# A four-layer graph network on one core: layer 3's algebra on VectorE, its sums in two passes, tests of adj moved

## The chip, the core and the metric

The kernel runs on one core of one Trainium2 chip. The core has five engines with instruction streams of their own: TensorE (PE: matrix products, with weight loads, PEld, beside them), VectorE (DVE), ScalarE (ACT), GpSimd (POOL) and SyncE (SP), which only starts transfers here. They meet through semaphores. Data lies in SBUF (128 partitions), products arrive in PSUM, inputs and outputs in device memory (HBM). The metric is the device time of one execution in microseconds (us); lower is better. A change counts as faster or slower when it moves the time by over 2%.

## The reference

Four layers over 4096 nodes of 64 features, each `x = x + layer(relu(layernorm(x)), adj)`. `adj` is 4096 x 4096 with about one entry in 128 set. Cut to what matters:

```python
# layer 0: a sum over the last 100 neighbours of each row, with weights that halve
rank = cumsum(mask, axis=1);  k = minimum(deg, 100);  pos = rank - (deg - k)
out0 = (mask * where(pos > 0, 0.5 ** (k - pos), 0)) @ (h @ weight) + bias
# layer 1: attention over neighbours in hyperbolic space
att = adj * sigmoid((2 + 2 * qm @ k.T) / att_scale + att_bias)
support = att @ h;  out1 = support / sqrt(clip(abs(-inner), 1e-8))
# layer 2: two gated steps (GRU), relu after each
m = adj @ (x @ W);  gi = m @ wih.T + bih;  gh = x @ whh.T + bhh
r = sigmoid(i_r + h_r);  z = sigmoid(i_z + h_z);  n = tanh(i_n + r * h_n)
x = relu((1 - z) * n + z * x)
# layer 3: a midpoint in the Poincare ball
XW = tanh(|mx| / |x| * artanh(|x|)) * mx / |mx|            # mx = x @ W
gamma = 2 / maximum(1 - sum(XW * XW), 1e-15)
num = A @ (gamma * XW);  den = A @ (gamma - 1)
mid = mobius_scalar_mul(0.5, num / den)
AXW = mobius_scalar_mul(sum(A, 1), mid)     # tanh(r * artanh(|x|)) * x / |x|
out3 = expmap0(relu(logmap0(AXW)))          # tanh(|u|) * u / |u|,  artanh(|y|) * y / |y|
```

## The kernel before

The fast path holds adj as one-byte floats in SBUF (`A8`, loaded and converted once, in layer 0, by transfers that GpSimd issues), and is right only if adj holds nothing but 0 and 1. So beside the layers it reads all of adj a second time in four-byte form and tests it, 256 blocks of 128 x 512; the number of other values becomes a flag, and if it is above 0 a slower general kernel runs afterwards.

The rows are worked on in four blocks `q` of 1024. Each engine works in program order, so the Python program plans the order itself: `Weave` keeps a book of estimated times. Products of the streams are emitted directly; the small work between layers and the tests are generators that yield one operation at a time, and after every few products `draw` issues those that the book holds ready. `work` (two pieces at a time) goes before `back` (the tests).

```python
    def pieces(self):
        return self.work[:self.width] + ([] if self.quiet else self.back)
    def force(self):
        piece = min(self.work[:self.width] or self.back, key=lambda p: self.begin(p[1]))
        self.issue(piece)
        self.draw(False)
    # in Engine.run(), when a transfer is started: its landing time in the book
    w.at[k] = max(w.t[self.e], w.t["P"]) + (8.0 if "whole" in k else 6.0 if "half" in k else 4.0), "S"
```

The tests load "halves" (128 x 512) or "wholes" (128 x 1024). `depth[0]` is how many are in flight: 1 in layer 0, 4 from layer 1; `spare[0]` allows wholes from layer 2.

```python
    def checks():
        ... # load up to depth[0] ahead; then for each block
            yield DV.scalar_tensor_tensor(a, a, 0.0, a, op0=ALU.not_equal, op1=ALU.not_equal,
                                          accum_out=odd[:, j:j + 1])
```

In layer 0 (`stream0`) TensorE counts neighbours into PSUM (`cnt`); ScalarE takes one half of every count, VectorE the other (`w`), and TensorE sums with these weights (`acc`). `root[0]` names the engine of the small statistics, GpSimd for blocks 0 to 2 and VectorE for the last. Layer 1 (`stream1`) makes scores, their sigmoid on ScalarE and the product with adj on VectorE (`sig`). Layer 2 has two steps (`layer2`), each closed by `gates`, whose end is on GpSimd:

```python
        yield GP.tensor_tensor(xT, xT, r, ALU.subtract)
        yield GP.tensor_tensor(xT, xT, z, ALU.mult)
        yield GP.tensor_tensor(xT, xT, r, ALU.add)
        yield AC.activation(xT, xT, AF.Relu)
```

After the second step `post2b` turns the result back (`ps_o`), adds it to `X[q]` and goes on to `pre3`, layer 3's source: layernorm (`h`), transpose (`ps_t`), product with W (`ps_l`), lengths, artanh, tanh, gamma, and three two-byte parts of each row's source in `S3`. Its artanh is half a logarithm, and for small arguments a polynomial on GpSimd:

```python
    def artanh(x):
        nb = x.shape[1]
        xc = stat("axc", nb)
        yield DV.tensor_scalar(xc, x, ARTANH_BOUND, None, op0=ALU.min)
        r = stat("at", nb)
        yield DV.tensor_scalar(r, xc, -1.0, 1.0, op0=ALU.mult, op1=ALU.add)
        q = yield from recip(r)
        yield DV.scalar_tensor_tensor(q, xc, 1.0, q, op0=ALU.add, op1=ALU.mult)
        low = small.tile([P, 2 * QB], I32, tag="st", name="flow")[:, :nb]
        yield DV.tensor_scalar(low, xc, 0.25, None, op0=ALU.is_lt)
        x2, p = stat("x2", nb), stat("po", nb)
        yield GP.tensor_tensor(x2, xc, xc, ALU.mult)
        yield AC.activation(q, q, AF.Ln)
        yield GP.tensor_scalar(p, x2, 1.0 / 13, 1.0 / 11, op0=ALU.mult, op1=ALU.add)
        for k in (9, 7, 5, 3, 1):
            yield GP.tensor_tensor(p, p, x2, ALU.mult)
            yield GP.tensor_scalar(p, p, 1.0 / k, None, op0=ALU.add)
        yield GP.tensor_tensor(p, p, xc, ALU.mult)
        yield DV.tensor_scalar(q, q, 0.5, None, op0=ALU.mult)
        yield DV.copy_predicated(q, low, p)
        return q
```

Layer 3's sums run over 32 blocks of columns for eight groups `u` of 512 rows; quarter `k` of the sum needs source `k`. `take3` brings a group's three parts together, `post3` closes one or two groups.

```python
    def layer3():
        late = NB - QB
        first = (0, 1, 2)
        for u in first:
            if u == 2:
                weave.until(("gates", NQ - 1), DONE)
            for k in range(NQ - 1):
                weave.until((4, k), DONE)
                sum3(u, k * QB, k * QB + QB)
        weave.until((4, NQ - 1), DONE)
        for us in ((0, 1), (2, 3), (4, 5), (6,), (7,)):
            for u in us:
                sum3(u, late if u in first else 0, NB)
            weave.add(post3([(u, take3(u)) for u in us]))
        weave.finish()
    def post3(parts3):
        nb = CB * len(parts3)
        ss, den, alpha = stat("ss", nb), stat("den", nb), stat("alpha", nb)
        part = [slice(i * CB, (i + 1) * CB) for i in range(len(parts3))]
        for h, (u, (n65, al)) in zip(part, parts3):
            sq = b2("sq")[:, :CB, :]
            yield AC.activation(sq, n65[:, :, :D], AF.Square)
            yield AC.activation(den[:, h], n65[:, :, D], AF.Copy)
            yield AC.activation(alpha[:, h], al, AF.Copy)
            yield DV.tensor_reduce(ss[:, h], sq, AX.X, ALU.add)
        sgn, a = stat("sgn", nb), stat("abs", nb)
        yield DV.tensor_scalar(sgn, den, 0.0, 2.0, op0=ALU.is_ge, op1=ALU.mult)
        yield DV.tensor_scalar(a, den, -1.0, DEN_EPS, op0=ALU.mult, op1=ALU.max)
        yield DV.tensor_tensor(den, den, a, ALU.max)
        n, nr = yield from lengths(ss)
        r = yield from recip(den)
        yield DV.tensor_tensor(n, n, r, ALU.mult)
        a = yield from artanh(n)
        yield DV.scalar_tensor_tensor(a, a, 0.5, alpha, op0=ALU.mult, op1=ALU.mult)
        yield DV.tensor_scalar(a, a, ARTANH_MAX, -ARTANH_MAX, op0=ALU.min, op1=ALU.max)
        yield DV.tensor_tensor(a, a, nr, ALU.mult)
        yield DV.scalar_tensor_tensor(a, sgn, -1.0, a, op0=ALU.add, op1=ALU.mult)
        for h, (u, (n65, al)) in zip(part, parts3):
            v = n65[:, :, :D]
            yield DV.tensor_tensor(v, v, rows(a[:, h]), ALU.mult)
            yield AC.activation(v, v, AF.Relu)
            sq = b2("sq")[:, :CB, :]
            yield AC.activation(sq, v, AF.Square)
            yield DV.tensor_reduce(ss[:, h], sq, AX.X, ALU.add)
        n, nr = yield from lengths(ss)
        yield DV.tensor_scalar(n, n, TANH_CLAMP, None, op0=ALU.min)
        yield AC.activation(n, n, AF.Tanh)
        yield DV.tensor_tensor(n, n, nr, ALU.mult)
        for h, (u, (n65, al)) in zip(part, parts3):
            v = n65[:, :, :D]
            yield DV.tensor_tensor(v, v, rows(n[:, h]), ALU.mult)
            x = X[u // 2][:, (u % 2) * CB:(u % 2 + 1) * CB, :]
            yield DV.tensor_tensor(x, x, v, ALU.add)
            yield SY.dma_start(out_nm[:, u * CB:(u + 1) * CB, :], x)
```

The main program ends with the tests that are left, then the flag, and the read of it in all engines (after the fast kernel, and before the branch to the general one):

```python
    layer3()
    while weave.back:
        weave.force()
    ... # flag_ps = odds summed over partitions, one product
    V.tensor_copy(flag, flag_ps[:1, :1])
            ...
            others = nc.values_load(flag)
            with tc.If(others > 0):
                general_kernel(tc, aps, out)
```

## Time and profile before

| what | value |
|---|---|
| time, median of 3 (lowest, highest) | 899.12 us (898.83, 900.8) |
| profiled execution: span, mean granted clock of TensorE | 897.3 us, 0.965 |
| layer 0, layer 1, layer 2 (from the rows "acc", "sig") | to 253, to 513, to 734 us |
| layer 3: last source complete, last product, end | 794.9, 857.9, 897.3 us |
| tests: halves in layers 0, 1, 2 | 21, 38, 7 |
| tests: wholes up to 735 us, to 797, to the end | 65, 16, 14 |
| read from HBM | 144.75 MB |

In the rows of the profile a line of the program is named by L and its number; since helpers record every operation, nearly all are L762 (VectorE, ScalarE, GpSimd) or L929 (products), and the tiles' names tell them apart: `A` is adj in one byte, `S` layer 3's source, `xT` the state in the gates, `po` the polynomial, `n` a group in the closing, `whole` and `half` the tests. "out<-in" gives what is written and read; the bracket at the end of a timeline row is the idle time before it and what ended it.

### The profile page before, as it was taken

Reading aid. Unit: us, or ns where it says so; the run is one execution under the profiler, and the core shown is the slowest. Engines: PE = TensorE matmul, PEld = TensorE weight load, DVE = VectorE, ACT = ScalarE, POOL = GpSimd, SP = SyncE. Lnnn points to the kernel's source line nnn. Section 1 sums busy time; section 2 is a strip of 40 time slices with the busy share of each in tenths; the row PEclk is TensorE's granted clock in tenths of the full one; section 3 lists DMA queues with packets and bytes.
Section 4 is the critical chain, followed back from the end, with each engine's and each line's share of the span. In section 5 each row is a group of like instructions: output and inputs, shape, how many; then the busy total and the mean of one; then the engine's idle time right before and its main releaser. Section 6 shows DMA issues by size and latency. Waiting matters only on the chain.

```text
span 897.3 us, 12837 instructions
## 1 busy us (share of the span) xinstructions
PE 812.4 (91%) x4682; PEld 383.4 (43%) x4682; DVE 657.2 (73%) x1456; ACT 369.1 (41%) x548; POOL 206.7 (23%) x470
## 2 busy tenths in 40 slices
PE   5999999999999999999999999899999974799920
PEld 2444444444433333333333344344444432789920
DVE  6755566665678888888888876577758788787776
ACT  4443444443455666666666510321103434322331
POOL 4342553556200000000000000422203363433121
PEclk9999999999999999999999999999999997799975
DMA  9997999999411320310311338477592432453210
GB/s 133 113 114 105 100 93 147 116 117 122 79 60 35 119 70 5 102 60 24 105 48 59 100 113 299 161 244 235 194 304 85 132 95 70 141 189 100 90 36 15
DMA packets 61702, 101.62 MB, mean 113 GB/s; under 512 B 18112, under 2 KB 34496, under 8 KB 61632
## 3 DMA queue, kind: packets, MB, share of 16 engines
q1 hardware_dynamic: 40752, 79.18, 28.4%
q0 software_dynamic: 18432, 16.79, 21.7%
q10 hardware_dynamic: 2448, 4.76, 1.4%
q8 instruction: 39, 0.64, 0.3%
q14 instruction: 31, 0.25, 0.1%
HBM read 144.75 MB, written 6.29 MB: 168 GB/s over the span
## 4 chain that ended last, share of the span: by engine, by line
PE 50%; DVE 14%; POOL 8%; ACT 3%; issue 3%; DMA 1%; POOLq 0%; DVEq 0%; ACTq 0%
PE acc L929 28%; PE score L929 13%; PE cnt L929 3%; POOL xT L762 3%; POOL po L762 3%; DVE nt L762 2%; DVE whole L762 2%; PE ps_l L929 2%; DVE ss L762 2%; DVE sig L762 1%; DVE n L762 1%; PE ps_n L929 1%; DVE ny L762 1%; PE ps_t L933 1%; POOL s3v L762 1%
## 5 line engine op out<-in xcount | busy, mean ns | idle before, releaser
L762 ACT ACTIVATE sig<-score,fatt_add,fatt_mul 128x1024 f32<-128x1024 f32 x128 | 147.6, 1200 | 84.1 <-PE score L929 84.0
L762 DVE TENSOR_TENSOR sig<-sig,A 128x1024 f32<-128x1024 f32 x128 | 151.4, 1222 | 34.6 <-ACT sig L762 34.0
L762 DVE TENSOR_SCALAR w<-cnt 128x512 int16<-128x512 f32 x128 | 88.5, 691 | 68.3 <-PE cnt L929 65.2
L762 DVE SCALAR_TENSOR_TENSOR whole<-whole 128x1024 f32<-128x1024 f32 x95 | 126.7, 1363 | 12.8 <-DMA whole<-in_adjT 12.4
L929 PE MATMUL score<-qd,kT 64*128 64x512 f32 x512 | 127.7, 616 | 0.7 <-ACT sig L762 0.4
L762 ACT ACTIVATE w<-cnt 128x512 int16<-128x512 f32 x128 | 76.4, 597 | 124.3 <-PE cnt L929 123.9
L762 POOL TENSOR_TENSOR xT<-xT,r 128x512 f32<-128x512 f32 x16 | 28.2, 1761 | 422.2 <-ACT r L762 421.7
L929 PE MATMUL acc<-sig,S 128*64 128x512 f32 x512 | 124.9, 606 | 0.3
L929 PE MATMUL acc<-A,hm 128*128 128x512 fp8e4 x512 | 117.5, 380 | 0.0
L929 PEld LDWEIGHTS <-hm 128*128 128x128 bf16 x768 | 72.3, 98 | 95.5 <-issue 17.9
L929 PE MATMUL cnt<-A,ftri 128*128 128x512 fp8e4 x256 | 98.0, 385 | 7.8 <-DMA A<-in_adjT 7.8
L929 PE MATMUL cnt<-A,fupd 128*128 128x512 fp8e4 x248 | 95.6, 386 | 5.0 <-ACT w L762 3.5
L929 PE MATMUL acc<-S,A 128*128 128x196 bf16 x1024 | 91.4, 251 | 4.9 <-POOL S L762 4.0
L929 PEld LDWEIGHTS <-A 128*128 128x128 fp8e4 x1024 | 89.5, 98 | 7.1 <-issue 6.6
L1073 POOL DMA_DIRECT2D A<-in_adjT x128 | 70.0, 559 | 48.5 <-DMA A<-in_adjT 45.6
L929 PEld LDWEIGHTS score<-qd,kT 64*128 64x128 f32 x512 | 43.9, 186 | 77.9 <-ACT sig L762 36.1
L929 PE MATMUL acc<-w,hm 128*128 128x512 bf16 x256 | 75.5, 379 | 0.0
L929 PEld LDWEIGHTS acc<-sig,S 128*64 128x64 f32 x512 | 30.4, 136 | 82.2 <-issue 31.2
L929 PE MATMUL acc<-A,lo 128*64 128x512 fp8e4 x512 | 61.3, 382 | 0.0
L929 PEld LDWEIGHTS <-lo 128*64 128x64 bf16 x768 | 35.6, 109 | 59.8 <-issue 39.6
L762 DVE SCALAR_TENSOR_TENSOR half<-half 128x512 f32<-128x512 f32 x66 | 44.0, 685 | 0.0
L929 PEld LDWEIGHTS <-fupd 128*128 128x128 bf16 x248 | 24.5, 99 | 43.5 <-issue 22.4
(194 smaller groups left out, 795.0 us busy)
## 6 DMA issues: line engine op xcount, KB each, us to landing
whole<-in_adjT SPq DMA_DIRECT2D x95, 512.0 KB, 5.4
half<-in_adjT SPq DMA_DIRECT2D x66, 256.0 KB, 3.0
A<-in_adjT POOLq DMA_DIRECT2D x128, 128.0 KB, 9.9
x<-in_x SPq DMA_DIRECT2D x8, 256.0 KB, 13.2
qs<-qd ACTq DMA_DIRECT2D x8, 256.0 KB, 5.1
qd<-qs SPq DMA_DIRECT2D x8, 256.0 KB, 2.7
mx<-gs SPq DMA_DIRECT2D x16, 128.0 KB, 6.9
xT<-gs SPq DMA_DIRECT2D x8, 256.0 KB, 6.4
```

The lines of the kernel that those rows point to most:

```text
L762: return fn(*args, **kw)
L929: nc.tensor.matmul(o, lhsT, rhs, start=start, stop=stop, skip_group_check=True)
L933: nc.tensor.transpose(o, src, ident)
L1073: nc.gpsimd.dma_start(A8[q][b // 2][:, b % 2, :], adjT[b * P:(b + 1) * P, q * 2 * CW:(q + 1) * 2 * CW])
```

## The change

It moves the work of GpSimd after layer 0's loads to VectorE: small statistics (`root[0]` stays VectorE), the end of the gates, artanh's polynomial (now of five coefficients and fused operations), and the last products of the sources. It puts table loads of ScalarE ahead of their use (`preload`). It gives the tests more transfers in flight (four halves in layer 0; four wholes and three halves from layer 2), books transfers as one queue, and holds the tests off (`quiet`) from the end of layer 2 until the second pass of the sums. Layer 3's sums go in two passes: three groups take sources 0 and 1 and are taken out of PSUM, three others take all four sources as they come, then the first three take sources 2 and 3 and the halves are added, and the last two follow alone. The closing uses that the relu can be applied before the lengths, and that expmap0 of logmap0 keeps directions: both lengths are computed at once and one chain is left of two. The flag is computed and read before the last chain is finished. It is meant to fill TensorE's waits and to shorten the closing.

```diff
         self.banks[self.kind.pop(k)].append(self.used[k][0])
+
+    def land(self, k, dur):
+
+        self.dma = max(self.dma, self.t["P"]) + dur
+        self.at[k] = self.dma + 2.4, "S"
 ...
-    def force(self):
-
-        piece = min(self.work[:self.width] or self.back, key=lambda p: self.begin(p[1]))
+    def force(self, back=False):
+
+        piece = min(self.work[:self.width] + (self.back if back else []), key=lambda p: self.begin(p[1]))
         self.issue(piece)
         self.draw(False)
 ...
+    depth = [4]
+    spare = [0]
 
     def checks():
 ...
-                if spare[0] and todo:
+            while todo or halves:
+                whole = sum(a.shape[1] > CW for a in loaded)
+                if whole < spare[0] and todo:
                     b, c = todo.pop(0)
                     load(b4p.tile([P, 2 * CW], F32, tag="b4", name="whole"), b, 2 * c, 2)
-                else:
+                elif len(loaded) - whole < depth[0]:
                     if not halves:
                         b, c = todo.pop(0)
                         halves += [(b, 2 * c), (b, 2 * c + 1)]
                     load(b2("half", (P, CW)), *halves.pop(0), 1)
+                else:
+                    break
             a, j = loaded.pop(0), n % 16
             n += 1
             yield DV.scalar_tensor_tensor(a, a, 0.0, a, op0=ALU.not_equal, op1=ALU.not_equal,
 ...
 
-                if c == 0:
+                if c == 0 or b % 2 == 0:
                     S_.activation(wt[:, cols[c]], cnt[c], AF.Relu, scale=-128.0)
                 else:
 ...
             for bs in pieces[-1:] if q < 2 else pieces:
                 sum2(accs[q], layer, q, bs)
+            if step and q == NQ - 1:
+                weave.quiet = True
             take2(q, step, accs.pop(q))
             weave.add(post(q))
 ...
         free(rz[0])
         yield AC.activation(r, r, AF.Tanh, bias=gb[:, 2:3])
-        yield GP.tensor_tensor(xT, xT, r, ALU.subtract)
-        yield GP.tensor_tensor(xT, xT, z, ALU.mult)
-        yield GP.tensor_tensor(xT, xT, r, ALU.add)
-        yield AC.activation(xT, xT, AF.Relu)
+        yield DV.tensor_tensor(xT, xT, r, ALU.subtract)
+        yield DV.tensor_tensor(xT, xT, z, ALU.mult)
+        yield DV.tensor_tensor(xT, xT, r, ALU.add)
         return xT
 ...
         ps = yield PE([o], run, 0.6, [kind])
-        yield DV.tensor_tensor(X[q], X[q], blocks(ps), ALU.add)
+        yield DV.scalar_tensor_tensor(X[q], blocks(ps), 0.0, X[q], op0=ALU.max, op1=ALU.add)
         free(ps)
         yield from pre3(q, kind)
 ...
 # artanh2 (artanh's lines are printed above; new order of Ln and the polynomial)
         q = yield from recip(r)
         yield DV.scalar_tensor_tensor(q, xc, 1.0, q, op0=ALU.add, op1=ALU.mult)
+        yield AC.activation(q, q, AF.Ln)
+        yield from preload(AF.Tanh)
         low = small.tile([P, 2 * QB], I32, tag="st", name="flow")[:, :nb]
         yield DV.tensor_scalar(low, xc, 0.25, None, op0=ALU.is_lt)
         x2, p = stat("x2", nb), stat("po", nb)
+        yield DV.tensor_tensor(x2, xc, xc, ALU.mult)
+        yield DV.tensor_scalar(p, x2, *(2.0 * c for c in ARTANH_POLY[:2]), op0=ALU.mult, op1=ALU.add)
+        yield DV.tensor_tensor(p, p, x2, ALU.mult)
+        for c in ARTANH_POLY[2:-1]:
+            yield DV.scalar_tensor_tensor(p, p, 2.0 * c, x2, op0=ALU.add, op1=ALU.mult)
+        yield DV.scalar_tensor_tensor(p, p, 2.0 * ARTANH_POLY[-1], xc, op0=ALU.add, op1=ALU.mult)
+        yield from between
         yield DV.copy_predicated(q, low, p)
         return q
 
 ... # pre3: preload(AF.Ln) before the lengths; its four GP operations are DV
 # layer3, summed (layer3 of before is printed above)
     def layer3():
+
+        half = NB // 2
+        sets = (0, 1, 2), (3, 4, 5)
+        early = {}
+        for k in range(2):
+            for place, u in enumerate(sets[0]):
                 weave.until((4, k), DONE)
+                sum3(u, place, k * QB, k * QB + QB)
+                if k:
+                    early[u] = take3(u)
+        for lo, hi in ((0, 1), (1, 2), (2, 3), (3, 4)):
+            for place, u in enumerate(sets[1]):
+                weave.until((4, lo), DONE)
+                sum3(u, place, lo * QB, hi * QB)
+                if hi == NQ:
+                    summed(u, take3(u))
+        weave.quiet = False
+        for place, u in enumerate(sets[0]):
+            sum3(u, place, half, NB)
+            summed(u, take3(u, early.pop(u)))
+        for place, u in enumerate((6, 7)):
+            sum3(u, place, 0, NB)
+            summed(u, take3(u), alone=True)
+        while weave.back:
+            weave.force(True)
+        others = nc.values_load(flag)
         weave.finish()
+        return others
+
+    pair = []
+
+    def summed(u, parts3, alone=False):
+        pair.append((u, parts3))
+        if alone or len(pair) == 2:
+            weave.add(post3(pair[:]))
+            pair.clear()
 ...
+        if more is not None:
+            V.tensor_tensor(n65, n65, more[0], ALU.add)
+            V.tensor_tensor(alpha, alpha, more[1], ALU.add)
 ... # post3, the new lines only
+        sgn, den, ss = stat("sgn", nb), stat("den", nb), stat("ss", 2 * nb)
+        vs = [n65[:, :, :D] for u, (n65, al) in parts3]
+        for h, v, (u, (n65, al)) in zip(part, vs, parts3):
+            d = n65[:, :, D]
+            yield DV.tensor_scalar(sgn[:, h], d, 0.0, 2.0, op0=ALU.is_ge, op1=ALU.mult)
+            yield DV.scalar_tensor_tensor(v, rows(sgn[:, h]), -1.0, v, op0=ALU.add, op1=ALU.mult)
+            sq = b2("sq")
+            yield AC.activation(sq[:, :CB, :], v, AF.Square)
+            yield DV.scalar_tensor_tensor(sq[:, CB:, :], v, 0.0, v, op0=ALU.max, op1=ALU.mult)
+            yield DV.tensor_scalar(den[:, h], d, -1.0, DEN_EPS, op0=ALU.mult, op1=ALU.max)
+            yield DV.tensor_tensor(den[:, h], den[:, h], d, ALU.max)
+            yield DV.tensor_reduce(ss.rearrange("p (k b) -> p k b", k=2)[:, :, h],
+                                   sq.rearrange("p (k b) d -> p k b d", k=2), AX.X, ALU.add)
+        yield from preload(AF.Ln)
+        rd = yield from recip(den)
+        n, r = yield from lengths(ss)
+        t = stat("t", nb)
+        yield DV.tensor_tensor(t, n[:, :nb], rd, ALU.mult)
+        ratio = stat("ratio", nb)
+        def between():
+            yield DV.tensor_tensor(ratio, n[:, nb:], r[:, :nb], ALU.mult)
+            for h, v in zip(part, vs):
+                yield DV.scalar_tensor_tensor(v, v, 0.0, rows(r[:, nb:][:, h]), op0=ALU.max, op1=ALU.mult)
+        a = yield from artanh2(t, between())
+            yield DV.scalar_tensor_tensor(a[:, h], a[:, h], 0.25, al, op0=ALU.mult, op1=ALU.mult)
+        yield DV.scalar_tensor_tensor(a, a, ARTANH_MAX, ratio, op0=ALU.min, op1=ALU.mult)
+        yield AC.activation(a, a, AF.Tanh)
+        for h, v, (u, (n65, al)) in zip(part, vs, parts3):
+    weave.dma = 5.2
 ...
-        root[0] = GP if q < NQ - 1 else DV
-    spare[0] = True
+    depth[0], spare[0] = 3, 4
 ... # flag_ps, its product and copy move to the end of checks()
+    others = layer3()
+    return others
```

## The prediction

> **What bounds the kernel now.** I read the busy shares and the forty slices first, to see which stage is not filled; then a table by stage; then, where TensorE is not filled, its instructions in order of time, and after its last product VectorE's. On the page:
>
> ```profile
> PE 812.4 (91%) x4682; PEld 383.4 (43%) x4682; DVE 657.2 (73%) x1456; ACT 369.1 (41%) x548; POOL 206.7 (23%) x470
> PE   5999999999999999999999999899999974799920
> DVE  6755566665678888888888876577758788787776
> PEclk9999999999999999999999999999999997799975
> DMA  9997999999411320310311338477592432453210
> ```
>
> TensorE is at 9 until slice 32 (layers 0, 1 and the first part of layer 2), so nothing there can bring much unless it shortens TensorE's own work, and the change does not. It falls to 7, 4, 7 at about 720 to 790 us and to 2, 0 in the last 40 us. The clock row falls with it. The same four stages as a table (layer 2; layer 3's sources; its sums; the closing):
>
> ```profile
> 513.00:734.00 221.00, 212.89 (x1234) 93.39 (x1232) 156.54 (x322) 50.38 (x81) 52.29 (x61) 0.99 0.58 188
> 734.00:797.00 63.00, 39.92 (x363) 35.07 (x362) 52.38 (x138) 20.59 (x38) 28.11 (x48) 0.81 0.38 125
> 797.00:858.00 61.00, 60.81 (x713) 60.55 (x711) 44.11 (x183) 18.68 (x61) 13.26 (x39) 1.00 0.36 116
> 858.00:897.30 39.30, 0.19 (x2) 0.11 (x2) 26.45 (x127) 10.89 (x21) 5.71 (x26) 0.55 0.07 15
> ```
>
> Columns after the length: busy time of TensorE, weight loads, VectorE, ScalarE, GpSimd, then clock, DMA share, GB/s. TensorE idles 23 us of 63 in the sources and is slowed besides (clock 0.81), is full in the sums, and has nothing in the last 39 us. So there are two holes. The first, in TensorE's own order:
>
> ```profile
> 754.12 1.11 PE L933 MATMUL ps_o<-fident,xT 128*128 128x128 f32 x4 [5.34 <-ACT xT L762]
> 765.79 1.11 PE L933 MATMUL ps_t<-fident,h 128*128 128x128 f32 x4 [10.56 <-DVE h L762]
> 768.12 0.81 PE L929 MATMUL acc<-S,A 128*128 128x196 bf16 x4 [1.22 <-POOL S L762]
> ```
>
> It waits for the chain of the last block of rows (q=3): gates, layernorm, source. The chain of waits there alternates between VectorE and GpSimd, with tests of adj ("whole") in between. The page names GpSimd's part:
>
> ```profile
> L762 POOL TENSOR_TENSOR xT<-xT,r 128x512 f32<-128x512 f32 x16 | 28.2, 1761 | 422.2 <-ACT r L762 421.7
> L762 DVE SCALAR_TENSOR_TENSOR whole<-whole 128x1024 f32<-128x1024 f32 x95 | 126.7, 1363 | 12.8 <-DMA whole<-in_adjT 12.4
> ```
>
> The second hole is the closing: after TensorE's last product at 857.9 two chains run almost one after the other, to the last update of X at 885.7, and only then come the last tests, the flag and the read of it:
>
> ```profile
> 885.27 0.42 DVE L762 TENSOR_TENSOR X<-X,n 128x256 f32<-128x256 f32 x1
> 889.44 1.22 DVE L762 SCALAR_TENSOR_TENSOR whole<-whole 128x1024 f32<-128x1024 f32 x1
> 891.45 0.15 DVE L762 CAST flag<-flag_ps 1x1 int32<-1x1 f32 x1 [0.37 <-PE flag_ps L1656]
> ```
>
> From the last X to the end (897.3) are 11.6 us: 5.2 of tests, 0.7 of flag, 5.7 for reading the flag in every engine and the branch.
>
> **What the Trainium skill says.** "SBUF — State Buffer", section Who interferes with whom: a VectorE instruction with two SBUF inputs and a GpSimd instruction that reads SBUF share one port pair, and one waits for the other's whole length; tensor_scalar can take the pair too, in its two-port modes. The trace agrees: a test takes 1.22 us when GpSimd is still and up to 2.28 beside it (748.7 us), one 16-element tensor_scalar on VectorE takes 1.26 instead of 0.17 (752.2 us), GpSimd's small ones 1.1 to 1.3 instead of 0.2. "ScalarE: Activation LUTs", section What ACT_TABLE_LOAD costs: a change of table set takes about 1283 ns. The trace has 1.28 us for each, some of them in front of a Tanh that a chain waits for. "TensorE: Matmul & The Clock Gate", section What's actually happening: an idle array falls to half clock. The clock here is 0.81 in the sources and 0.55 in the closing.
>
> **The change part by part.**
>
> *Layers 0 and 1 (to 513 us).* In layer 0 half of VectorE's evictions of the counts (64 of 0.69 us) go to ScalarE (0.60 each), and the small statistics of three blocks of rows come from GpSimd to VectorE, some 47 operations of 0.2 us each block: -33 us (the three blocks with tests) and +28, even. TensorE is full (182.6 busy of 186 us from 67 to 253), so the length stays. What changes is the tests: 21 halves there now, one in flight; with four in flight I estimate 30 more. VectorE idles 73 us of those 186, and 30 take 30x0.69=21. For DMA: A's tiles follow each other every 1.25 us where nothing else loads (GpSimd's issues from 42 to 57 us), and TensorE uses one each 1.83 us, so a half (about 0.62 by its size) fits into two blocks of three and more. Layer 1 has VectorE at 220 of 260 us and keeps its 38 halves. Sum: 0, give or take 3 us.
>
> *Layer 2 (513 to 734).* The gates' three operations leave GpSimd (1.27 to 2.1 us each) for VectorE (0.69, as its other 128x512 ones): about 3 us less in each of eight chains. TensorE waits on that result 4.9 us (ps_l) and 2.4 (ps_o before 740); I take 4 back, so the sums end near 730. VectorE idles 65 us here; gates for seven chains take 7x3x0.69=14.5, the first two sources some 12. Half of the remaining 38, at 1.23 a test, is 15 more tests. So of the 30 "whole" now tested after 735 us, 15 are gained in layer 0 (30 halves) and perhaps 11 to 15 here; I take four as left, 5 us.
>
> *Layer 3's sources.* The chain of q=3 takes from 734 to 794.9 us now (last S part). In the new one I count: take and gates 6.7 us, GRU end 2.1, ps_o and X 1.3, layernorm 5.6, transpose, product and copies 2.7, squares 2.0, lengths 2.4, artanh with its polynomial (7x0.2 instead of 13 GpSimd steps of 0.3) 2.6, tanh to factors 2.3, S 3.2. Sum 31; with another block's operations between, 35. No tests are in it. So the last source is ready near 765.
>
> *The sums.* TensorE has 1024 products at 88.8 ns (216 in 19.17 us) = 91 us, plus 9 us for projections and transposes. Before, three groups waited for sources 0 to 2 before the first could be closed; now three groups take the first two sources, three others all four as they come: 17+25=42 us of products that do not need q=3. From 730 that is work until 781, later than 765. The hole closes, and TensorE ends near 730+9+91=830 instead of 857.9.
>
> *The closing.* A pair's algebra is 36 small operations at 0.2 us and per half six large ones (five of 0.44, one of 0.70): 7.2+5.8=13.0 us of VectorE. Before: 42 small ones and 4.3 large, 12.7. It is the chain that is shortened (one chain of lengths, no GpSimd polynomial, no second Square), not VectorE's work. A single group is about 9.3, eleven takings with their additions 10.5. Sum: 3x13.0+2x9.3+10.5=68 us, which start when group 3 is complete, at 730+9+17+34-5.7=784. That gives 852, against 830+1.6+10.5=842 from TensorE's end. VectorE, not TensorE, sets the end. Some of it overlaps: before, 53.8 us were busy where this count gives 58 (0.17 for 0.2), so 63 to 68: 847 to 852. I take 850.
>
> *The end.* Tests left 5, waiting for the flag in the last chain 2, and after the last X its output and the branch 4 to 5 (an estimate: of the 11.6 now, without tests and most of the read). 850+5+2+5=862.
>
> **The rivals.** (1) Tests stay over: if layer 0's loads find less room, VectorE in the tail gets up to 15 tests more, 18 us: 880. For it: the DMA share is already 0.87 there. Against: the 1.25 us above. (2) Layer 0's larger test loads delay A's tiles and TensorE waits: 5 to 10 us, 870. Against: tiles are issued twelve ahead and land in 9.9 us, the twelve last 22. GpSimd with no arithmetic left also issues them in time. (3) Banks: the last chains need one and two-bank buffers that the new groups hold from their start; if gates of q=3 come after the third group has taken its bank they wait 17 us, the hole stays, 878. Against: TensorE's first two groups last 5.7 us and the gates are ready 2.2 us after the sums. (4) VectorE overlaps better than counted, and no test is left: TensorE's end plus the last chain bounds, 842+5: 848.
>
> **Range and chances.** 862 is 4.1% below the time before, on the profile's scale; the timed median is 1.8 above its span, inside my error. The low end is rival 4, the high end rival 1 or 3 in full: 848 to 880. Faster by over 2% means under 881: 0.85; the rest is two rivals together: same 0.11, slower 0.04.
>
> **What would show it.** Right: TensorE without a wait over 2 us between 730 and 830 and clock near 1 there; no GpSimd arithmetic; VectorE near full from 785 to the end; the flag's copy before the last X. Wrong: a long wait of TensorE for h or xT after 740 (step of the sources), "A" among TensorE's waits in layer 0, over ten tests after 785, or VectorE with much idle in the closing (then its chains, not its work, set the end).

## The result and the profile after

| | before | after |
|---|---|---|
| time, median (lowest, highest) | 899.33 us (898.83, 900.8), 4 runs | 848.85 us (848.38, 850.1), 4 runs |
| ratio, 95% interval | | 0.9438 (0.9422 to 0.9455) |
| profiled span, granted clock of TensorE | 897.3 us, 0.965 | 846.8 us, 0.988 |
| TensorE: products of layer 1 end, of layer 2, of layer 3 | 514.3, 734.0, 857.8 us | 516.6, 727.5, 821.8 us |
| last source complete, last update of X starts | 793.7, 885.3 us | 771.5, 839.6 us |
| tests left when the closing starts or later | 14 wholes that end after 797 us | 1 whole, 1 half |

The kernel is 50.5 us faster: 36.0 us up to the end of TensorE's products, and 14.5 us after it. (The last source of before is complete at 793.7 us; the 794.9 of the table of before is 1.2 us too late.) The page first, its busy line and the forty slices:

```profile
PE 803.9 (95%) x4682; PEld 378.5 (45%) x4682; DVE 644.0 (76%) x1670; ACT 397.8 (47%) x609; POOL 69.5 (8%) x143
PE   5999999999998999999999999999999999999980
DVE  6725766667667888888888888977678788885996
PEclk9999999999999999999999999999999999999995
DMA  9999999999641041032022133796778920000010
```

The hole at slices 33 to 35 is gone, TensorE is at 9 from slice 14 to slice 38, and its clock falls only in the last slice. GpSimd fell from 206.7 us of busy time to 69.5, nearly all in layer 0. VectorE is not busier than before (644.0 against 657.2 us) although it took over GpSimd's work: 64 evictions of layer 0 went to ScalarE (397.8 us busy against 369.1), and the tests became shorter. DMA moves its load to slices 26 to 32, where four wholes are in flight.

By stage: layer 2, the sources beside the first sums, the closing beside the last sums, and what follows TensorE's last product (columns as before):

```profile
513.00:728.00 215.00, 213.60 (x1255) 94.08 (x1252) 171.56 (x418) 52.06 (x87) 0.46 (x4) 1.00 0.63 206
728.00:777.00 49.00, 48.98 (x540) 46.07 (x538) 36.02 (x136) 21.67 (x48) 0.48 (x4) 1.00 0.01 2
777.00:822.00 45.00, 44.83 (x527) 44.60 (x524) 38.91 (x179) 17.12 (x52) 0.00 (x0) 1.00 0.06 14
822.00:846.80 24.80, 0.19 (x2) 0.09 (x2) 16.59 (x83) 7.28 (x15) 0.00 (x0) 0.59 0.10 25
```

TensorE lacks 0.02 us of 49 and 0.17 of 45. The last 24.8 us are what remains of the second hole. TensorE's own order, where the three waits of before (5.34, 10.56 and 1.22 us) stood:

```profile
740.88 0.60 PE L951 MATMUL ps_o<-fident,xT 128*128 128x128 f32 x4
...
749.14 0.60 PE L951 MATMUL ps_t<-fident,h 128*128 128x128 f32 x4
...
752.54 69.29 PE L947 MATMUL acc<-S,A 128*128 128x196 bf16 x812
840.31 0.19 PE L947 MATMUL flag_ps<-fones,odds 128*1 128x1 f32 x2 [18.48 <-DVE odds L780]
```

No row has a bracket until the flag's product. 812 products in 69.29 us are 85.3 ns each. The two groups that stood for GpSimd and for the tests (the first from the tile's view: durations as lowest, median and highest ns, then first and last start):

```profile
L780 DVE TENSOR_TENSOR xT<-xT,r x16: 675/692/693, 566.5 to 739.0; 128x512 f32<-128x512 f32 x16
```

```profile
L780 DVE SCALAR_TENSOR_TENSOR whole<-whole 128x1024 f32<-128x1024 f32 x53 | 63.5, 1219 | 4.9 <-DMA whole<-in_adjT 4.3
```

The gates' operation takes 0.69 us where it took 1.76 on average on GpSimd. A whole test takes 1.22 us on average where it took 1.36. The shorter test fits what the Trainium skill says in "SBUF — State Buffer", section Who interferes with whom: a VectorE instruction with two SBUF inputs, as the test is, contends with a GpSimd instruction that reads SBUF. The run gates_pool below puts such instructions back and shows the difference. Last, VectorE around the closing:

```profile
770.62 0.83 DVE L780 TENSOR_TENSOR S<-s3v,S 128x260 bf16<-128x260 f32 x2
777.29 0.62 DVE L780 TENSOR_TENSOR n<-n,acc 128x130 f32<-128x130 f32 x2 [5.84 <-ACT alpha L780]
...
835.34 1.22 DVE L780 SCALAR_TENSOR_TENSOR whole<-whole 128x1024 f32<-128x1024 f32 x1
...
838.50 0.68 DVE L780 SCALAR_TENSOR_TENSOR half<-half 128x512 f32<-128x512 f32 x1
...
839.56 0.42 DVE L780 TENSOR_TENSOR X<-X,n 128x256 f32<-128x256 f32 x1
...
840.54 0.15 DVE L780 CAST flag<-flag_ps 1x1 int32<-1x1 f32 x1 [0.28 <-PE flag_ps L947]
```

Three things are to be seen. VectorE has nothing to do for 5.84 us just before the closing starts. Two tests lie in the middle of the last chain. The flag's copy comes after the last X, so the read of the flag is not ahead of anything.

### The profile page after: what moved, and what is told of

Same layout as the page of the kernel before. It is cut to its first block, busy times and chain, and to the rows that moved or that the text cites. A ratio compares the mean times of both kernels' runs of the same rounds, so it can differ in the third digit from the quotient of the medians.

```text
span 846.8 us, 12798 instructions
## 1 busy us (share of the span) xinstructions
PE 803.9 (95%) x4682; PEld 378.5 (45%) x4682; DVE 644.0 (76%) x1670; ACT 397.8 (47%) x609; POOL 69.5 (8%) x143
## 4 chain that ended last, share of the span: by engine, by line
PE 86%; DVE 7%; DMA 2%; ACT 2%; issue 1%; POOL 0%; POOLq 0%; ACTq 0%; DVEq 0%
PE acc L947 50%; PE score L947 14%; PE cnt L947 13%; PE ps_l L947 2%; PE ps_t L951 2%; PE rz L947 2%; DMA half<-in_adjT 2%; PE ps_n L947 2%; PE ih L947 1%; DVE sig L780 1%; DVE n L780 1%; DVE nt L780 1%; DMA A<-in_adjT 1%; PE ps_kq L947 1%; DVE rc L780 1%
## 5 line engine op out<-in xcount | busy, mean ns | idle before, releaser
L780 ACT ACTIVATE w<-cnt 128x512 int16<-128x512 f32 x192 | 108.1, 595 | 95.9 <-PE cnt L947 93.8
L780 DVE SCALAR_TENSOR_TENSOR half<-half 128x512 f32<-128x512 f32 x150 | 98.3, 683 | 2.6 <-DMA half<-in_adjT 2.6
L947 PE MATMUL acc<-S,A 128*128 128x196 bf16 x1024 | 88.5, 247 | 0.0
L947 PEld LDWEIGHTS <-A 128*128 128x128 fp8e4 x1024 | 87.2, 97 | 1.5 <-issue 1.0
L780 DVE TENSOR_SCALAR w<-cnt 128x512 int16<-128x512 f32 x64 | 44.2, 690 | 50.9 <-PE cnt L947 49.8
L1104 POOL DMA_DIRECT2D A<-in_adjT x128 | 67.7, 531 | 138.5 <-DMA A<-in_adjT 135.1
L780 DVE SCALAR_TENSOR_TENSOR whole<-whole 128x1024 f32<-128x1024 f32 x53 | 63.5, 1219 | 4.9 <-DMA whole<-in_adjT 4.3
## 6 DMA issues: line engine op xcount, KB each, us to landing
A<-in_adjT POOLq DMA_DIRECT2D x128, 128.0 KB, 12.7
```

The source lines that it names most:

```text
L780: return fn(*args, **kw)
L947: nc.tensor.matmul(o, lhsT, rhs, start=start, stop=stop, skip_group_check=True)
L1104: nc.gpsimd.dma_start(A8[q][b // 2][:, b % 2, :], adjT[b * P:(b + 1) * P, q * 2 * CW:(q + 1) * 2 * CW])
```

## The experiments

Each one alters the changed kernel unless it says otherwise. The ratios are to the kernel before, timed on the same chip; the differences in us are to 848.85 (the kernel before differs by up to 0.5 us between these chips). The first six put one part of the change back, or give it to the engine that had it.

### one_pass: the sums in the order of before

```diff
-        for k in range(2):            # groups 0-2: sources 0, 1; groups 3-5: all four; ...
+        for u in (0, 1, 2):           # groups 0-2: sources 0, 1, 2; then each group to its end
+            ... sum3(u, place(u), k * QB, k * QB + QB)   # k = 0, 1, 2
+        weave.quiet = False           # after the last source
+        for us in ((0, 1), (2, 3), (4, 5), (6,), (7,)): ...
```

> The changed kernel with the order of layer 3's sums of before: groups 0 to 2 take sources 0 to 2, then all wait for source 3, then (0,1), (2,3), (4,5), 6, 7. Everything else as changed. Theory 'order' (the two passes fill TensorE): group 0 has only 5.7 us of products before it needs source 2, which is complete at 761, so TensorE idles about 20 us between 741 and 761 and the time is 868 to 874. Rival 'chains' (the sources are now so quick that any order is filled): TensorE idles under 6 us and the time is under 855.

Measured: 855.15 us, ratio 0.9504 (0.9488 to 0.9519), +6.3 us. The hole is back in TensorE's order:

```profile
739.77 0.63 PE L951 MATMUL ps_o<-fident,xT 128*128 128x128 f32 x4 [0.61 <-DVE xT L780]
751.68 6.45 PE L947 MATMUL acc<-S,A 128*128 128x196 bf16 x40 [11.28 <-DVE S L780]
...
776.10 0.19 PE L947 MATMUL flag_ps<-fones,odds 128*1 128x1 f32 x2
776.22 61.80 PE L947 MATMUL acc<-S,A 128*128 128x196 bf16 x724
```

TensorE ends at 838.0, 16 us later, yet the time grows by only 6.3. What came between is seen after TensorE's end: here the last X ends at 848.4, 10.4 us after the last product; in the changed kernel it ends 18.2 us after it. With TensorE late, VectorE has no backlog (45.0 us busy of the 61 before TensorE's end), and the last group's chain runs alone: 40 operations are left after 838.0. So in the changed kernel some 8 us of the tail are a queue in front of VectorE, that is, work of earlier groups that it still has to do, and among it 1.9 us of tests. The two-pass order closes the hole, and the queue takes back more than half of it. The expectation for the order was too high for two reasons: TensorE's waits for the sources are 12.3 us (1.01 and 11.28) and not about 20, and it counted the hole without the queue.

### gates_pool: the end of the gates on GpSimd

```diff
-        yield DV.tensor_tensor(xT, xT, r, ALU.subtract)   # and the two after it
+        yield GP.tensor_tensor(xT, xT, r, ALU.subtract)
```

> The changed kernel with the three last operations of the gates on GpSimd again (relu stays fused). Theory: each chain of layer 2 gets 2 to 4 us longer and tests that run beside GpSimd get slower; TensorE waits again for xT, 4 to 6 us in layer 2, and source 3 comes 3 us later, which its slack of 3.4 us (complete at 771.5, used at 774.9) just takes: 853 to 857. Rival (VectorE is what layer 2 lacks, so freeing 17 us of it pays): more tests fit before 727, the time is 847 to 850.

Measured: 857.45 us, 0.9534 (0.9512 to 0.9557), +8.6. The tile's view and TensorE's order:

```profile
L780 POOL TENSOR_TENSOR xT<-xT,r x16: 1262/1346/2127, 566.2 to 746.8; 128x512 f32<-128x512 f32 x16
```

```profile
731.57 4.38 PE L947 MATMUL acc<-S,A 128*128 128x196 bf16 x48
...
783.63 48.84 PE L947 MATMUL acc<-S,A 128*128 128x196 bf16 x544 [4.07 <-DVE S L780]
```

The sums start 4.2 us later (727.4 in the changed kernel), and the last source comes too late even for the two-pass order, which then waits 4.07 us. In the changed kernel the last source is complete 3.9 us before TensorE uses it (771.5 and 775.4; the expectation has 3.4), so the order of sums and the faster gates need each other. The tests beside GpSimd get longer again, up to 2.28 us, where none before 735 us takes over 1.23 in the changed kernel:

```profile
L780 DVE SCALAR_TENSOR_TENSOR whole<-whole x53: 1206/1220/2280, 531.3 to 668.4; 128x1024 f32<-128x1024 f32 x53
```

The first half of the rival came true and did not help: more tests fit into layer 2, all are done by 672 us, and still the kernel is slower. The time is 0.5 us above what was expected.

### l3_pool: the polynomial and the last operations of the sources on GpSimd

```diff
-        yield DV.tensor_tensor(x2, xc, xc, ALU.mult)      # polynomial: 6 operations on VectorE
+        yield GP.tensor_tensor(x2, xc, xc, ALU.mult)      # 9 on GpSimd; also s3v and S
```

> The changed kernel with artanh's polynomial and the three products of the sources on GpSimd again. Theory 'work' (from 777 on VectorE's queue sets the end): the closing loses 5 x 7 small VectorE operations, 7 us, against a source 3 that is 5 us later: 845 to 851. Theory 'chain' (the end is TensorE's end plus the last chains, one after the other): every closing gets 1.5 to 2 us longer, the last two count, and the later source makes TensorE wait 2 us: 853 to 859.

Measured: 853.85 us, 0.9486 (0.9468 to 0.9504), +5.0. TensorE has two waits of 1.18 and 3.18 us for the gates' `r` and ends at 827.5, 5.6 us later. The second of them is, by the program, a wait for banks of PSUM: the third group's sums need two, and those of `ih` come free with the gates' last read of it into `r` (it ends at 741.92, and the sums go on at 741.97). The prediction's rival 3 had this the other way round, gates waiting for the group. VectorE's busy time after 777 us falls from 55.5 to 52.7 us, and the time still grows. So theory 'work' is out. Of theory 'chain' the time came true; most of it is TensorE's later end, and the distance from there to the last X grows only from 18.2 to 19.4 us.

### old_post3: the closing algebra of before

```diff
-        rd = yield from recip(den)
-        n, r = yield from lengths(ss)      # both lengths at once, one tanh
+        n, nr = yield from lengths(ss)     # two lengths, one after the other, two tanh
```

> The changed kernel with the closing algebra of before (two chains of lengths, two Squares and Relu on ScalarE), with the new artanh on VectorE. VectorE's count is nearly the same: 12.7 against 13.0 us a pair. Theory 'work': the end moves by less than 2 us: 847 to 851. Theory 'chain': a single group's chain is longer by one chain of lengths and three trips to ScalarE, about 5 us, and groups 6 and 7 follow one after the other at the end: 854 to 862.

Measured: 859.52 us, 0.9555 (0.9541 to 0.957), +10.7. TensorE ends at the same time. VectorE before and after TensorE's end, and a wait in the last chain:

```profile
777.00:822.00 45.00, 45.00 (x529) 44.58 (x526) 37.24 (x185) 19.93 (x69) 0.00 (x0) 1.00 0.06 14
822.00:857.90 35.90, 0.01 (x1) 0.00 (x0) 24.49 (x132) 10.81 (x25) 0.00 (x0) 0.57 0.07 17
```

```profile
848.12 0.42 DVE L780 TENSOR_REDUCE ss<-sq 128x4 f32<-128x256 f32 x1 [0.93 <-ACT sq L780]
```

VectorE is busy for 61.7 us after 777, 6.2 more than in the changed kernel, with 317 operations where that has 262. My count had put the old pair at 12.7 us and the new one at 13.0, and said that the new algebra shortens the chain and not VectorE's work. It does both: about 6 us are work, and the rest is put down to the longer chain with its waits for ScalarE, which no run separates further. (The old closing has no early table load for Ln either.)

### tests_slow: the tests at the pace of before

```diff
-    depth = [4]
+    depth = [1]                    # halves in flight, layer 0
-    depth[0], spare[0] = 3, 4
+    depth[0], spare[0] = 1, 4      # halves from layer 2
```

> The changed kernel with one half in flight in layer 0 and one half beside four wholes from layer 2; the hold-off in the sources stays. Theory 'work': about 40 halves fewer in layer 0, some made up in layer 2, so 12 to 20 wholes are left after 777, and each adds its 1.23 us to VectorE's queue: 863 to 873. Rival (VectorE has gaps in the closing that take them, or layer 2 takes them all): 848 to 853.

Measured: 877.37 us, 0.9761 (0.9743 to 0.9778), +28.5, the largest of all parts. The last X is at the same 839.6 us; behind it stand 15 wholes and 5 halves:

```profile
839.60 0.42 DVE L780 TENSOR_TENSOR X<-X,n 128x256 f32<-128x256 f32 x1
839.94 1.22 DVE L780 SCALAR_TENSOR_TENSOR whole<-whole 128x1024 f32<-128x1024 f32 x1
...
847.72 1.23 DVE L780 SCALAR_TENSOR_TENSOR whole<-whole 128x1024 f32<-128x1024 f32 x1 [2.10 <-DMA whole<-in_adjT]
...
868.07 0.15 DVE L780 CAST flag<-flag_ps 1x1 int32<-1x1 f32 x1 [0.28 <-PE flag_ps L947]
```

This is above all that was expected, and rival 1 of the prediction in full. A test that is left over adds more than its 1.22 us, because it waits for its transfer as well: the 20 tests are 21.8 us of work and take 27.4. The change avoids this by testing 64 halves in layer 0, where this run tests 28 and the kernel before 21.

### layer0_old: layer 0's division of work as before

```diff
-                if c == 0 or b % 2 == 0:
+                if c == 0:
                     S_.activation(wt[:, cols[c]], cnt[c], AF.Relu, scale=-128.0)
...
         acc = stream0(q)
+        root[0] = GP if q < NQ - 1 else DV
```

> The changed kernel with layer 0's division of work as before: VectorE takes the second half of every count out of PSUM (64 more evictions of 0.69 us than now, ScalarE 64 fewer), and the small statistics of three blocks of rows go back to GpSimd. If this part is only a shift of even size, as predicted, the time stays within 3 us of 848.9 and layer 0 ends within 1 us of where it ends now. Rival: it was made to give the tests room on VectorE; then layer 0 holds fewer halves than 64 (45 to 55), some five to nine wholes come back after 777 us, and the time is 853 to 860. A third: GpSimd's arithmetic delays the loads of A that it issues, TensorE waits for A in layer 0, and the time is 850 to 855.

Measured: 856.42 us, 0.9531 (0.9513 to 0.9548), +7.6. First the tile `cnt` in the changed kernel, then in this one, and this one's waits of TensorE up to 520 us (total, times, longest):

```profile
L947 PE MATMUL cnt<-A,ftri x256: 377/379/634, 7.9 to 247.0; 128*128 128x512 fp8e4 x128
```

```profile
L947 PE MATMUL cnt<-A,ftri x256: 377/379/634, 7.8 to 252.9; 128*128 128x512 fp8e4 x128
```

```profile
PE cnt L947 <- DMA A<-in_adjT: 7.8, 1, 7.8
PE ps_t L951 <- DVE S L780: 3.4, 3, 2.2
PE ps_t L951 <- DVE h L780: 3.1, 4, 0.9
```

The counts end 5.9 us later and layer 3's sums 4.5. The waits name VectorE's `S` and `h`, from which layer 1's sources are turned, and not transfers: for A there is only the one wait at the start. With 59 halves beside its old share of the work, VectorE is late with these. Three wholes and a half are left after 777 us, one of each behind the last X. The last X ends 5.1 us later and the end comes 9.4 us after it instead of 6.8. So the division isn't the even shift that I had made of it. Of the rival the time came true and the reason only in part: 59 halves fit and not 45 to 55, two wholes more than in the changed kernel came back and not five to nine, and the larger share of the loss is TensorE's delay of 4.5 us. The division pays for the tests: with 21 halves (the kernel before) the counts end at 246.2, with 59 and the old division at 252.9, with 64 and the new one at 247.0. before_tests agrees (60 halves, the old division: 250.6).

### before_tests: the kernel before with only the new pacing of the tests

```diff
-    depth = [1]
+    depth = [4]
...
+            if step and q == NQ - 1:
+                weave.quiet = True       # until the last source is complete
...
-    spare[0] = True
+    depth[0], spare[0] = 3, 4
```

> The kernel before with only the change's pacing of the tests (four halves in flight in layer 0, four wholes and three halves from layer 2, transfers booked as one queue, tests held off from the end of layer 2 until the last source is ready); the sources, the sums in one pass and the closing are those of before. If the tests are worth what tests_slow lost (28.5 us), it runs at 871 to 876. If their worth in the changed kernel came from its full VectorE after 777 us, where every test adds its length, while the kernel before has idle VectorE there, it gains only the tests after the last chain (5 us) and some waits of the sources' chain: 884 to 894. I expect between, 878 to 886, since 30 wholes of 37 us leave the part after 735 us, of which VectorE had about half idle.

Measured: 885.09 us, 0.9838 (0.9823 to 0.9853): 14.3 us gained on the kernel before (1.6%, under the 2% at which a change counts as faster), as expected between the two theories. No test is left after 680 us, but the two long waits of the sources are there:

```profile
752.48 1.12 PE L938 MATMUL ps_o<-fident,xT 128*128 128x128 f32 x4 [4.26 <-ACT xT L767]
764.17 1.11 PE L938 MATMUL ps_t<-fident,h 128*128 128x128 f32 x4 [10.57 <-DVE h L767]
...
768.71 81.22 PE L934 MATMUL acc<-S,A 128*128 128x196 bf16 x952
```

The wait for `h` was 10.56 us with tests in the chain and is 10.57 without them. The tests were never its cause; gates_pool and one_pass show that the chain and the order of the sums decide over such waits. The short waits of that stretch do go with the tests: those for `S` fall from 4.0 to 0.4 us in all, and the last source is complete at 784.5 instead of 793.7. The part alone gains 14.3 us, and tests_slow loses 28.5 us by giving back only the number of halves in flight. Late tests cost more in the changed kernel: there 15 wholes and 5 halves lie behind the last X, while in the kernel before 26 of 30 late wholes lie beside the sources and the closing, and four behind the last X.

### no_tests: all 256 tests left out

```diff
-        todo = [(b, c) for c in range(NQ) for b in range(NB)]
+        todo = []
```

The flag is then always 0; the kernel leaves out the test of adj, and only that.

> The changed kernel without any test of adj (left out: the 256 blocks are neither loaded nor tested; the flag is 0). Theory: the tests now cost only what stands in the last chains and behind the flag, 3 us, and up to 2 us by which layer 1 starts later: 843.5 to 846.5. Rival (the loads and tests still slow layers 0 to 2): 838 to 842.

Measured: 842.08 us, 0.9362 (0.9348 to 0.9377), -6.8. TensorE's last product starts 5.6 us earlier (816.0) and the last X 6.5 us earlier. That lies between the two theories. All 256 tests, 161.8 us of VectorE, cost 6.8 us: they lie almost wholly beside other work, and most of what they cost is small delays of TensorE in layers 0 to 2 (the sums start at 721.7 instead of 727.4). The end comes 6.9 us after the last X here, although the flag is copied at 129 us.

### early and early_late: the tests let on before the last quarter of the sums, the flag read ahead of the last chain or behind it

```diff
# early
+                weave.quiet = hi < NQ
                 sum3(u, place, lo * QB, hi * QB)
# early_late: this, and
-        others = nc.values_load(flag)
         weave.finish()
+        others = nc.values_load(flag)
```

> The changed kernel, but the tests are let on again from source 3 on (before the last quarter of groups 3 to 5) instead of after it: VectorE idles 5.8 us there, at 771 to 777. Theory: the last 1.5 tests leave the last chains (1.9 us), the flag is read during the sums, and what follows the last X shrinks from 6.8 to about 5.4 us, as in the run with one pass, where the flag also came early: 844.5 to 847. Rival (VectorE in the closing has room for the tests, and the end is bound by the output's transfer): no change, 848 to 849.5.

> As 'early', but the flag is read by the engines after the last chain, as before the change: this shows what the read ahead is worth by itself once the tests are done in time. From the spans so far (5.7 us from flag to end before, 5.4 to 5.9 from the last X to the end where the flag was early) the read costs 0.5 to 2 us more than the output's transfer and the branch: 1 to 2 us above 'early'. Rival (the whole 5.7 us come after the chain): 3 us or more above it.

Measured: early 846.44 us (846.2 to 848.31), 0.9416 (0.9403 to 0.9429), -2.4; early_late 846.52, 0.9411 (0.9398 to 0.9424). In early the idle time of VectorE takes the two tests:

```profile
771.25 1.22 DVE L780 SCALAR_TENSOR_TENSOR whole<-whole 128x1024 f32<-128x1024 f32 x1
...
772.39 0.69 DVE L780 SCALAR_TENSOR_TENSOR half<-half 128x512 f32<-128x512 f32 x1
...
775.88 0.15 DVE L780 CAST flag<-flag_ps 1x1 int32<-1x1 f32 x1 [2.39 <-PE flag_ps L947]
```

The last chain is rid of the tests, the last X starts 0.8 us earlier (838.74), and the end comes 5.4 us after it instead of 6.8. Where the flag is read makes no difference (0.08 us): the 1 to 2 us that I expected of it aren't there. What is left as the gain is that tests and flag are done before the last X. How much of the 1.4 us behind the last X is the flag stays open, since no_tests has 6.9 us there with an early flag.

### turns and best1: the queue taken away

turns lets two closings that lie beside each other issue one operation each in turn, with 30 small buffers instead of 24 (what the buffers do by themselves wasn't tried). best1 does that, lets the tests on as early does, and completes groups 3 and 4 before group 5 takes its third and fourth source.

```diff
# turns
+        w = self.work[:self.width]
+        if self.turns and len(w) > 1 and self.last is w[0]:
+            w.reverse()
# best1: this, and
+        for u, lo in ((3, 0), (4, 0), (5, 0), (3, 1), (4, 1), (5, 1), (3, 2), (4, 2), (3, 3), (4, 3), (5, 2), (5, 3)):
+            weave.quiet = weave.quiet and lo < NQ - 1
```

> The changed kernel with turns alone: two closings beside each other take one operation each. If dependent starts (0.2 us apart against 0.08) are what fills VectorE in the closing, the time falls by 2 to 5 us, to 844 to 847. If the book's order already mixes two closings well enough, 848 to 850, no difference.

> The changed kernel with three things more: the tests let on again once the last source is ready (as in early), groups 3 and 4 completed before group 5 so that the first closing can start about 3 us of sums earlier and VectorE's idle time at 771 to 777 us is filled, and two closings that lie beside each other take turns, one operation each, since independent small operations start closer together than dependent ones. If the backlog of VectorE's work is what holds the end (the lone last chain took 10.4 us in one_pass, and it ends 18.2 us after TensorE in the changed kernel), each of these takes from it: 838 to 844 us, with the last X 11 to 14 us after TensorE's last product. The floor from TensorE's end, a lone chain and the 5.4 us of the end is about 839.6. Rival: the backlog is made by the takings and by PSUM banks, which the order of operations doesn't change: 845 to 847, as early (846.4). A third: taking turns delays the older pair, whose buffers and output then come later, and the last chain waits for it: 847 to 852.

Measured: turns 845.23 us (844.94 to 845.61), 0.9396 (0.9381 to 0.941), -3.6; best1 840.65 us (839.84 to 842.7), 0.9347 (0.9335 to 0.936), -8.2. How turns gains is seen in VectorE's order. First the changed kernel, then turns:

```profile
802.59 0.18 DVE L780 SCALAR_TENSOR_TENSOR nt<-nt,ss 128x16 f32<-128x16 f32 x1
802.80 0.17 DVE L780 SCALAR_TENSOR_TENSOR ny<-nt,guess 128x16 f32<-128x16 f32 x1
803.01 0.17 DVE L780 TENSOR_TENSOR nt<-ny 128x16 f32<-128x16 f32 x1
```

```profile
803.30 0.17 DVE L788 SCALAR_TENSOR_TENSOR ny<-nt,guess 128x16 f32<-128x16 f32 x1
803.38 0.16 DVE L788 TENSOR_SCALAR den<-n 128x4 f32<-128x4 f32 x1
803.50 0.17 DVE L788 TENSOR_TENSOR nt<-ny 128x16 f32<-128x16 f32 x1
803.60 0.16 DVE L788 TENSOR_TENSOR den<-den,n 128x4 f32<-128x4 f32 x1
```

Operations that need each other start 0.21 us apart. One that doesn't need its neighbour starts 0.08 to 0.12 us after it, so the other closing's small operations cost next to nothing in the gaps. The Trainium skill measures otherwise for longer operations: in "VectorE: DVE Perf Modes", section The DRAIN you can't avoid, eight copies take 13.88 us (1.7 us each, by division) with a wait after each, and just as long with one only after the last. For operations of 0.17 us the measurement here decides: the wait for the neighbour's result is worth 0.1 us each time. Of turns' gain the last X shows 1.7 us (it starts at 837.84); the other 1.4 lie behind it, where the flag's copy no longer stands (835.41), as in early. In best1 the stretches before and after TensorE's end:

```profile
777.00:824.00 47.00, 46.91 (x551) 46.48 (x548) 40.87 (x194) 18.28 (x52) 0.00 (x0) 1.00 0.08 18
824.00:840.50 16.50, 0.00 (x0) 0.00 (x0) 9.57 (x61) 5.87 (x13) 0.00 (x0) 0.65 0.09 22
```

VectorE has 9.6 us of work after TensorE's end, where the changed kernel has 16.6. The last X ends 11.1 us after the last product (18.2 in the changed kernel); the lone chain of one_pass took 10.4. In this profile TensorE ends 2 us later than in the changed kernel. The queue is gone, and the chain of the last group is what is left. Early's 2.4 us and turns' 3.6 both hold the same 1.4 us behind the last X, so they make 4.6 together, and best1's 8.2 leave about 3.6 for the new order of the groups (an estimate, if the parts add up); that order wasn't run alone. best1 is the fastest kernel that does the whole computation.

## Why the prediction was right, and which of its terms were off

**The step from 899 to 862 us held in direction and mechanism**; the result lies 13 us lower, only 0.85 us above the low end of the range (848). All five terms of the sum were off, four of them the same way, so the range held by little. On the profile's scale 862 stands against 846.8 (and is 3.9% below the 897.3 us of before; the 4.1% of the prediction mixes the two scales):

| term | predicted | measured | difference |
|---|---|---|---|
| the closing starts | 784 | 777.3 | -6.7 |
| VectorE's closing, tests taken out | 66 | 60.8 | -5.2 |
| tests left | 5 | 1.9 | -3.1 |
| waiting for the flag in the last chain | 2 | 0 | -2.0 |
| after the last X | 5 | 6.8 | +1.8 |
| end | 862 | 846.8 | -15.2 |

*Start of the closing.* The sums start at 727.4 instead of 730: 6.6 us earlier than layer 2 ended before, where I had counted 4, although layer 1 ends 2.3 us later. gates_pool gives 4.2 of them back, so the gates were sized rightly; where the other part comes from wasn't isolated. A product took 85.3 ns and not 88.8, a figure from a stretch of 216. The products of other kinds between the sums took 7 us (94.4 us in all, less 1024 x 85.3 ns) and not 9. The same three terms bring TensorE's end to 821.8, where I had 830.

*The sources.* Predicted ready near 765, measured 771.5. The chain was sized too short: it takes 44 us from the start of the sums and not 35. That did no harm, as TensorE needed the last source only at 775.4. gates_pool shows how thin that reserve is.

*The closing.* That VectorE and not TensorE sets the end was right, though it was busy for 38.9 of the 45 us before TensorE's end and so not quite "near full". one_pass shows the queue from one side and best1 from the other. The size was 5.2 us too large. 3.1 us of that are a slip of the sum: it counts all eleven takings into the closing, but three of them, of the first pass, lie before it (743.6 to 751.6 us; the last is shown).

```profile
750.75 0.88 DVE L780 TENSOR_TENSOR n<-n,acc 128x260 f32<-128x260 f32 x2 [0.26 <-ACT alpha L780]
```

The rest fits that a stretch of mixed operations is shorter than its number times 0.2 us, since independent ones start closer together. The prediction's remark that only the chain gets shorter was wrong (old_post3).

*The tests.* Four wholes were expected to be left; a whole and a half were. I expected 51 halves in layer 0, and there were 64. A term that I had set to nothing, the even division of layer 0, isn't nothing: it lets these 64 lie there without delay to TensorE (layer0_old). In the sum it stays at nothing only because the tests took what it freed.

*The flag.* The step that failed as a mechanism: its copy does not come before the last X. The tests were held off until the last chains had been planned, so both tests and flag landed among or behind them. early and early_late show that, with both done early, the place of the read is worth nothing that can be measured.

*The rivals.* Rival 1 (tests stay over) is real but didn't happen: tests_slow makes it happen, at 877. Rivals 2 and 3 left no trace in the changed kernel: no wait for A but the first, and no wait for a bank between 727 and 822 (l3_pool has one of 3.2 us, with the roles exchanged). Rival 4 came nearest by its number, 848, but for half its reason: hardly a test was left, while VectorE's queue still stood.

**What each part is worth.** Put back one at a time they cost 28.5 (pacing of the tests), 10.7 (closing), 8.6 (gates), 7.6 (layer 0), 6.3 (two passes) and 5.0 us (sources): 66.7 in sum, against 50.5 gained. More than the whole: the parts need each other, and one that is taken out spoils some of what the others gain. Without the fast gates the two-pass order waits again (4.07 us), without layer 0's new division its tests delay TensorE, and the pacing of the tests is worth 28.5 us here and 14.3 alone (there with the hold-off).

Open: best1's order of groups alone wasn't run. Nor was it tried which piece of layer 0's division counts, the evictions on ScalarE or the statistics off GpSimd. The early table loads of ScalarE and the hold-off of the tests (`quiet`) weren't put back alone either.

## What to carry to other kernels

Work that may lie anywhere (here 162 us of tests) is worth moving to where its engine idles early, even if that needs a shift of other work that looks even by itself; at the end every piece costs its full length and its transfer. When one hole is closed, look at once for the queue that forms behind it: the distance from the last product to the last output, compared with that of a lone chain, measures it. And two chains of small dependent operations belong on one engine in alternation, not one after the other.

## What the runs showed of the hardware

- On VectorE a small operation that depends on the one before starts 0.19 to 0.21 us after it, an independent one 0.07 to 0.12 us (changed kernel and turns, after 777 us).
- Four test loads in flight beside A's loads bring DMA in layer 0 to a share of 1.00 between 67 and 247 us (0.89 before), at 169 GB/s instead of 110, without one wait of TensorE for A after the first tile.
- From the end of the last X to the end of the execution it takes 5.4 to 5.9 us wherever the flag is read (early 5.4, one_pass 5.4, best1 5.5, early_late 5.9), and 6.8 us in the changed kernel, where the flag's copy comes behind the last X. no_tests is an exception, with 6.9 us and an early flag (one traced execution each).
- A table load of ScalarE takes 1.28 us; in the changed kernel the next activation starts 0.01 us after it for 20 of 22 loads.
